# Transposed input of the later pairs: loaded in a second layout and normalised in place, or transposed on TensorE

## The chip, the cores and the metric

The kernel runs on one core of a Trainium2 chip. The metric is the device time of one execution in microseconds (us). Everything is float32. A core has five engines that run their own instruction streams: TensorE (PE in the profile, PEld for its weight loads), VectorE (DVE), ScalarE (ACT), GpSimd (POOL) and SyncE (SP), which here only issues DMA transfers.

## The reference

One transformer block over x of shape (8, 256, 512): 2048 tokens, each a row of 512 numbers.

```python
x = x + attention(layernorm(x), w_qkv, w_o)   # 32 query heads, 8 key/value heads, head size 128
x = x + ffn(layernorm(x), weight, bias, centroids, assignments)

def layernorm(x):          # over the last axis, no learned scale
    return (x - mean(x)) / sqrt(var(x) + 1e-5)

def attention(h, w_qkv, w_o):
    q, k, v = split(h @ w_qkv)
    scores = q @ k.T * 128 ** -0.5 - slope[head] * sqrt(i - j)   # causal: -inf where j > i
    return softmax(scores) @ v @ w_o

def ffn(h, ...):
    hits = softmax(h @ centroids.T / 0.1) > 0.01                 # 64 clusters
    dense = h @ weight.T + bias
    return where(any(hits, axis=1)[:, None] & any(hits, axis=0)[assignments][None, :], dense, 0)
```

## The kernel before

The eight sequences of the batch are taken two at a time. A pair is 512 tokens, held as four tiles of 128 tokens; there are four pairs, 0 to 3. Inside a pair the work goes by key/value head and by sequence: 8 heads times 2 sequences are 16 units, called slots 0 to 15 here (`slot = u % SPP`). A unit u computes the scores of its own head group; in the same stretch of instructions the unit before it has its maximum subtracted, its exponential taken and its rows summed, and the unit two back is multiplied with v and projected with w_o. The order on every engine is written out by hand (`manual_schedule`): the two long lines with `qq`, `e`, `x`, `w`, `rows` and `norm` in the body of the unit loop are that order, one for even slots (`bb == 0`) and one for odd slots. All matrix products with weights use Strassen's seven products, so GpSimd and VectorE also form sums of weight blocks (`a_sums`, `b_sums`).

TensorE contracts over the partition axis, so the projections of q, k and v need x with its 512 features on the partitions: `xT[p]`, a tile of 128 partitions by 4 feature chunks by 512 tokens. Before the change it comes about like this, for pair p + 1 while pair p is being worked on:

- slot 8: `load_x2` brings the four token tiles of the pair from memory (SP queue);
- slots 10 and 11: `norm(0)` to `norm(3)` treat two token tiles each. `norm_stats` (L259, L260, VectorE) gives mean and variance of each token, `norm_root` (L267, ScalarE) and `norm_scale` (L272, L274, VectorE) give `rstd` and `shift = -mean * rstd`, each one column with a token on each partition, and `norm_write` (L281, ScalarE) writes the normalised tile `xn`;
- slots 11 and 12: `x(0)` and `x(1)` call `norm_tile`, which transposes one normalised tile: four TensorE transposes into one PSUM bank (L290) and a ScalarE copy to `xT` (L291). Each of the two slots does two tiles, one before and one after `w(1)`;
- slots 13 and 14: `sum_x` (L125 to L131, VectorE) forms the Strassen sums of `xT`; slot 14 and 15 use it for the first projections of the next pair.

Four other steps of the same slots matter here. `sum_old` (L387, L388, L390, VectorE) reduces the rows of the exponentials; it comes right after `x(...)` in VectorE's order. `rows` transposes that result on TensorE (`tp_r`, L397), reduces it (L401, L404, VectorE), writes it to memory (`row_hbm`, L406, SP queue) and reads it back on all partitions (`bc`, L415, SP queue, two transfers). `subtract_max` uses `bc` on GpSimd (L422) and VectorE (L425), and `attend` uses it on VectorE (L450) for the result of `av`. After `attend`, `a_sums` forms the sums of `oT` on GpSimd (`o_s`, L112 to L118); at the end of an odd slot GpSimd also sums the next weights (L112 to L116 of `wq`, L125 and L129 of `wo`), in an even slot it finishes `wq_s` (L118).

Pair 0 goes through its own code ahead of the loop and is not touched by the change.

Of the kernel before, what the change touches and what calls it, by code (L numbers as in the profile page):

```python
# [14 lines left out]
F32 = mybir.dt.float32  # L15
I32 = mybir.dt.int32
AF = mybir.ActivationFunctionType
ALU = mybir.AluOpType
# [3 lines left out]
B, S, H = 8, 256, 512  # L22
# [3 lines left out]
P = 128  # L26
NC_H = H // P
PT_TOK = 2 * S
NPAIR = B // 2
# [24 lines left out]
def block_kernel(  # L54
    ctx: ExitStack,
    tc: tile.TileContext,
    x: bass.AP,
    w_qkv: bass.AP,
    w_o: bass.AP,
    w_ffn_t: bass.AP,  # L60
# [6 lines left out]
    nc = tc.nc  # L67
# [7 lines left out]
    work = ctx.enter_context(tc.tile_pool(name="work", bufs=1))  # L75
    small = ctx.enter_context(tc.tile_pool(name="small", bufs=4))
    dram = ctx.enter_context(tc.tile_pool(name="dram", bufs=4, space=bass.MemoryType.DRAM))
# [11 lines left out]
    gp, ve = nc.gpsimd.tensor_tensor, nc.vector.tensor_tensor  # L89
# [17 lines left out]
    def a_sums(tt, a, which="S1 S2 S3 S4"):  # L107
        for s in which.split():
            if callable(a[s]):
                a[s] = a[s]()  # L110
            if s == "S1":
                tt(a["S1"], a["A21"], a["A22"], ALU.add)  # L112
            elif s == "S2":
                tt(a["S2"], a["S1"], a["A11"], sub)
            elif s == "S3":
                tt(a["S3"], a["A11"], a["A21"], sub)  # L116
            else:
                tt(a["S4"], a["A12"], a["S2"], sub)  # L118
# [56 lines left out]
    def load_x2(t):  # L175
        x2[t] = work.tile([P, H], F32, tag="x2", name=f"x2_{t}", bufs=X2_BUFS)
        nc.sync.dma_start(x2[t], xf[ts(t, P), :])
# [75 lines left out]
    def norm_stats(*tiles):  # L253

        n = len(tiles)
        mv = small.tile([P, 2, 2], F32, tag="mv", name="mv", bufs=2)[:, :n]
        for j, t in enumerate(tiles):
            stats = small.tile([P, 6], F32, tag="stats", name=f"stats_{t}")
            nc.vector.bn_stats(stats, x2[t])  # L259
            nc.vector.bn_aggr(mv[:, j], stats)  # L260
        return mv, tiles
# [24 lines left out]
    def transpose_into(dst, xn, t, tp=None, copy=nc.scalar.copy):  # L286
        if tp is None:
            tp = p_tp.tile([P, 512], F32, tag="tp", name=f"tpx_{t}")
        for c in range(NC_H):
            nc.tensor.transpose(tp[:, ts(c, P)], xn[:, ts(c, P)], ident)  # L290
        copy(dst, tp.rearrange("p (c q) -> p c q", c=NC_H))  # L291

    xT = {}
    xB = {}

    def norm_tile(p, i, **kw):

        if i == 0:
            xT[p] = work.tile([P, NC_H, PT_TOK], F32, tag="xT", name="xT", bufs=2)
        t = p * TPP + i  # L300
        transpose_into(xT[p][:, :, ts(i, P)], xn_sb[t], t, **kw)

    def sum_x(p, which):

        if p in xB:
            b_sums(ve, xB[p], which)
            return
        s = work.tile([P, 3, 2, S], F32, tag="xT_t", name="xT_t")
        xB[p] = b_side([xT[p][:, 2 * k : 2 * k + 2, ts(n, S)] for k in range(2) for n in range(2)],
                       *(s[:, j] for j in range(3)))  # L310
        b_sums(ve, xB[p], which)
# [12 lines left out]
    def project_k(p, j):  # L324

        kT = kT_sb[p, j] = work.tile([P, 2, PT_TOK], F32, tag="kT", name="kT", bufs=2)
        return strassen("k", "aw", wk[p, j], xB[p],
                        lambda w, x: [(slice(0, S), w[:, c, :], x[:, c, :]) for c in range(2)],
                        [kT[:, m, ts(n, S)] for m in range(2) for n in range(2)], S)

    def project_q(g):

        qT = qT_sb[g] = work.tile([P, G, PT_TOK], F32, tag="qT", name="qT", bufs=2)
        v = qT.rearrange("p (e m) t -> p e m t", m=2)
        return strassen("q", "aq", wq[g], xB[g // NKV],
                        lambda w, x: [(ts(e, S), w[:, c, e, :], x[:, c, :]) for e in range(2) for c in range(2)],
                        [v[:, :, m, ts(n, S)] for m in range(2) for n in range(2)], 512)
# [167 lines left out]
    def ffn_transpose(t, tag="xnT", **kw):  # L505
        xnT_sb[t] = work.tile([P, NC_H, P], F32, tag=tag, name=f"xnT_{tag}")
        transpose_into(xnT_sb[t], xn_sb[t], t, **kw)
# [119 lines left out]
    k, q = project_k(0, 0), project_q(0)  # L627
# [15 lines left out]
    found = None  # L643

    for u in range(NU + 2):
        g, bb = divmod(u, 2)
        p, kv = divmod(g, NKV)
        slot = u % SPP
        own, old, out_ = u < NU, 0 < u <= NU, u >= 2
        more_q, more_p = own and g + 1 < NG, own and p + 1 < NPAIR  # L650
# [14 lines left out]
        e, qq = nothing, nothing  # L665
        if own and slot in (0, 1, 8, 9):
            e = project_v(p, slot // 8, bb)
        elif own and slot in (3, 7, 11):
            e = project_k(p, (slot + 1) // 4)
        elif more_p and slot == 15:  # L670
            e = project_k(p + 1, 0)
        if more_q:
            if bb == 0:
                q = project_q(g + 1)
            qq = q
        ww = {}

        def w(*steps):
            for i in steps:
                if out_:  # L680
                    if i == 1:
                        ww[0] = project_out(u - 2)
                    ww[0](i)
# [8 lines left out]
        def f(part):  # L692
            if t_ffn is not None:
                if part == 0:
                    ffn_transpose(t_ffn)
                elif part == 1:
                    ffn_logits(t_ffn)
                    ffn_exp(t_ffn)
                    ffn_dense(t_ffn, w_ffn)
                elif part == 2:  # L700
                    ffn_bias_add(t_ffn, y_late[:, t_ffn % TPP, :] if t_ffn >= first_late else None)
                else:
                    ffn_hits(t_ffn)
                    ffn_qsel(t_ffn)
                    ffn_end(t_ffn)


        t_norm = None
        if more_p and slot in (10, 11):
            t_norm = (p + 1) * TPP + 2 * (slot - 10)  # L710
        elif own and p > 0 and slot in (2, 4) and p < NPAIR - 1:
            t_norm = (p - 1) * TPP + slot - 2
        elif u in (NU - 3, NU - 1):
            t_norm = (NPAIR - 2) * TPP + u - (NU - 3)

        def norm(part):
            nonlocal found
            if t_norm is not None:
                found = (lambda _: norm_stats(t_norm, t_norm + 1), norm_root, norm_scale, norm_write)[part](found)

        def max_and_old():
            scores(u, 2)
# [14 lines left out]
        def sum_old():  # L737
            if old:
                over_keys(s_sb[u - 1], r, 1, ALU.add)
# [20 lines left out]
        def av(i):  # L760
            if out_:
                attend(u - 2, i)
                if i == 1:
                    a_sums(gp, o_sb[u - 2][1])

        def x(i):
            if more_p and slot in (11, 12):
                norm_tile(p + 1, 2 * (slot - 11) + i)

        if bb == 0 and own:  # L770
            qq(1), e(1), max_and_old(), e(2), f(0), av(0), e(6), exp_old(), av(1), more_sums(), rows_max(), f(1), e(7), qq(2)
            if u == 4:
                onehot_of_columns(asg)
            f(2), norm(0), e(5), e(4), qq(6), e(3), x(0), w(1), x(1), sum_old(), w(5, 6), norm(1), qq(7), w(2)
            rows(), behind_rows(), w(7, 3), norm(3), w(4)
        elif u < NU - 1:
            e(1), qq(4), e(2), max_and_old(), f(0), e(6), av(0), exp_old(), e(7), av(1), f(1), e(5), qq(5)
            f(2), norm(0), e(4), e(3), x(0), w(1), x(1), sum_old(), w(5, 6), norm(1), qq(3), w(2)
            rows(), behind_rows(), w(7, 3), norm(3), w(4)
        elif own:  # L780

            max_and_old(), f(0), av(0), exp_old(), av(1), rows_max(), f(1)
            f(2), norm(0), w(1), sum_old(), w(5, 6), norm(1), w(2)
            rows(), subtract_max(u, 0), subtract_max(u, 1)
            f(3), norm(2), w(7)
            nc.scalar.activation(s_sb[u], s_sb[u], AF.Exp)
            w(3), norm(3), w(4)
        elif bb == 0:
            sum_old(), av(0), av(1), f(0), rows(), f(1), w(1, 5), f(2), w(6, 2, 7, 3, 4), f(3)
        else:  # L790
            av(0), f(0), av(1), f(1)
            normalise(norm_stats(last, last + 1), tags=("y", "y"))
            ffn_hits(t_ffn), ffn_qsel(t_ffn)
            w(1), f(2), w(2, 5, 6)
            ffn_transpose(last)
            w(3)
            found = norm_root(norm_stats(last + 2))
            ffn_transpose(last + 1, "snap")
            w(7)
            norm_write(norm_scale(found))  # L800
            ffn_logits_product(last), ffn_logits_product(last + 1)
            w(4)
# [30 lines left out]
        if more_p and slot == 8:  # L833
            for i in range(TPP):
                load_x2((p + 1) * TPP + i)

        if u == 2:
            asg = load_assignments()
# [2 lines left out]
        if u == NU - 1:  # L841

            for i, (tag, pool) in enumerate((("xT", work), ("wq", wpool))):
                both = []
                for hbm in (x2_hbm[i], y_hbm[i]):
                    t = pool.tile([P, TPP, H], F32, tag=tag, name=f"back_{tag}", bufs=2)
# [45 lines left out]
    n = 0  # L892
    for t in range(NT):
        if t in SPLIT:
            continue
        p, i = divmod(t, TPP)
# [32 lines left out]
```

## Time and profile before

| | |
|---|---|
| median of 3 runs | 1440.6 us (1440.53 to 1444.04) |
| the profiled execution | 1441.13 us, its span 1439.4 us |
| TensorE busy | 1407.5 us, 98% of the span |
| VectorE busy | 928.2 us, 64% |
| GpSimd busy | 878.2 us, 61% |
| ScalarE busy | 372.2 us, 26% |
| granted TensorE clock, mean | 0.996 |
| DMA | 189.94 MB, 132 GB/s on average |

Busy time is the sum of the spans of an engine's instructions. Idle time of an engine that does not set the end costs nothing. A timeline row gives the start in us from the span's start, the time in us, the engine, the line of the kernel, the operation, what it writes and reads, the shapes, and in square brackets how long the engine had been idle before it and which instruction ended that.

### The profile page before, as it was taken

How to read it: one execution, taken by the hardware profiler on the slowest of the kernel's cores; microseconds unless marked ns; L12 is line 12 of the kernel's file. 1: busy time of each engine (PE TensorE's matmuls, PEld its weight loads, DVE VectorE, ACT ScalarE, POOL GpSimd, SP SyncE). 2: the span in 40 equal slices, each digit the busy share in tenths (PEclk: the TensorE clock that was granted, in tenths of full speed). 3: DMA queues.
4: the chain of work that ended last, by engine and by line, in shares of the span. 5: the costliest groups of instructions: out<-in, count | busy, mean ns of one | idle time of the engine just before them, and what ended most of it. 6: DMA issues, size and time to landing. Idle time of an engine off the chain costs nothing.

```text
span 1439.4 us, 16533 instructions
## 1 busy us (share of the span) xinstructions
PE 1407.5 (98%) x5859; PEld 1072.9 (75%) x5859; DVE 928.2 (64%) x1708; ACT 372.2 (26%) x650; POOL 878.2 (61%) x883
## 2 busy tenths in 40 slices
PE   8899999999999999999999999999999999999986
PEld 7677777767877777777777677787777777877663
DVE  5457666686556665667655666566756676556766
ACT  2222223411232222332213312142222211222332
POOL 6377857676464754667555466566747666466543
PEclk9999999999999999999999999999999999999998
DMA  5235433443242544424242425434323353243343
GB/s 190 88 122 176 132 115 136 146 147 132 89 161 74 176 144 150 161 98 142 98 147 102 167 83 176 153 126 147 132 90 117 132 176 132 89 162 103 101 149 117
DMA packets 85968, 189.94 MB, mean 132 GB/s; under 512 B 10592, under 2 KB 18784, under 8 KB 85888
## 3 DMA queue, kind: packets, MB, share of 16 engines
q1 hardware_dynamic: 84736, 186.41, 37.5%
q10 hardware_dynamic: 864, 1.57, 0.3%
q8 instruction: 47, 0.77, 0.2%
q0 software_dynamic: 288, 0.92, 0.2%
q14 instruction: 33, 0.27, 0.1%
HBM read 175.77 MB, written 13.11 MB: 131 GB/s over the span
## 4 chain that ended last, share of the span: by engine, by line
PE 90%; DVE 6%; issue 1%; ACT 1%; POOL 1%; DMA 1%; DVEq 0%; POOLq 0%; ACTq 0%; SPq 0%
PE ps_qa L145 14%; PE ps_oa L468 14%; PE ps_oc L468 7%; PE sc L370 7%; PE ps_qc L145 7%; PE av L446 7%; PE sc L376 4%; PE ps_ob L468 4%; PE ps_ka L145 4%; PE ps_va L145 4%; PE av L447 3%; PE ps_qb L145 3%; PE ps_f L546 3%; PE ps_kc L145 2%; PE ps_vc L145 2%
## 5 line engine op out<-in xcount | busy, mean ns | idle before, releaser
L500 POOL TENSOR_TENSOR x<-x,snap 128x256 f32<-128x256 f32 x189 | 136.0, 736 | 177.5 <-DVE x L488 105.1
L422 POOL TENSOR_TENSOR s<-s,bc 128x1024 f32<-128x1024 f32 x64 | 151.7, 2370 | 150.2 <-DMA bc<-row_hbm 150.0
L387 DVE TRANSPOSE_TENSOR_REDUCE r<-s 128x32 f32<-128x1024 f32 x128 | 158.0, 1234 | 4.5 <-ACT s L735 4.5
L112 POOL TENSOR_TENSOR o_s<-oT 128x256 f32<-128x256 f32 x64 | 47.6, 744 | 180.3 <-DVE oT L450 176.3
L158 ACT COPY qT<-ps_qa 128x512 f32<-128x512 f32 x128 | 74.8, 584 | 289.7 <-PE ps_qa L145 289.6
L483 ACT COPY snap<-ps_oa 128x256 f32<-128x256 f32 x189 | 70.4, 373 | 277.8 <-PE ps_oa L468 277.8
L468 PE MATMUL ps_oa<-wo,oT 128*128 128x256 f32 x512 | 132.7, 381 | 2.6 <-DVE oT L450 2.6
L735 ACT ACTIVATE s<-s 128x1536 f32<-128x1536 f32 x63 | 93.5, 1484 | 148.5 <-DVE s L425 137.8
L446 PE MATMUL av<-s,v 128*128 128x512 f32 x256 | 130.7, 592 | 0.0
L145 PE MATMUL ps_qa<-xT,wq 128*128 128x256 f32 x512 | 121.1, 379 | 0.8 <-ACT qT L158 0.8
L370 PE MATMUL sc<-qT,kT 128*128 128x512 f32 x256 | 120.3, 592 | 0.0
L145 PEld LDWEIGHTS ps_qa<-xT,wq 128*128 128x128 f32 x512 | 97.1, 190 | 27.8 <-issue 16.0
L372 DVE SCALAR_TENSOR_TENSOR s<-sc,alibi 128x512 f32<-128x512 f32 x128 | 88.0, 691 | 30.8 <-PE sc L370 29.8
L468 PEld LDWEIGHTS ps_oa<-wo,oT 128*128 128x128 f32 x512 | 90.9, 190 | 22.6 <-DVE oT L450 5.3
L378 DVE SCALAR_TENSOR_TENSOR s<-sc,alibi 128x512 f32<-128x512 f32 x64 | 44.3, 692 | 85.6 <-PE sc L376 85.6
L447 PEld LDWEIGHTS av<-s,v 128*128 128x128 f32 x256 | 48.6, 190 | 61.2 <-issue 61.2
L450 DVE TENSOR_TENSOR oT<-av,bc 128x512 f32<-128x512 f32 x128 | 83.9, 683 | 11.8 <-PE av L447 10.5
L388 DVE TRANSPOSE_TENSOR_REDUCE r<-s 128x16 f32<-128x512 f32 x128 | 85.6, 669 | 0.0
L447 PE MATMUL av<-s,v 128*128 128x256 f32 x256 | 76.1, 379 | 0.0
L488 DVE TENSOR_TENSOR x<-x,ps_ob 128x256 f32<-128x256 f32 x64 | 26.9, 421 | 73.2 <-PE ps_ob L468 73.1
L370 PEld LDWEIGHTS sc<-qT,kT 128*128 128x128 f32 x256 | 48.6, 190 | 33.9 <-issue 29.9
L494 DVE TENSOR_TENSOR x<-x,ps_oc 128x256 f32<-128x256 f32 x128 | 53.3, 416 | 30.5 <-PE ps_oc L468 29.6
(182 smaller groups left out, 2982.0 us busy)
## 6 DMA issues: line engine op xcount, KB each, us to landing
bc<-row_hbm SPq DMA_DIRECT2D x128, 512.0 KB, 4.8
wq<-in_w_qkv SPq DMA_DIRECT2D x32, 1024.0 KB, 7.7
wo<-in_w_o SPq DMA_DIRECT2D x32, 1024.0 KB, 7.8
alibi<-al_hbm SPq DMA_DIRECT2D x24, 512.0 KB, 8.4
wk<-in_w_qkv SPq DMA_DIRECT2D x16, 512.0 KB, 9.4
wv<-in_w_qkv SPq DMA_DIRECT2D x8, 1024.0 KB, 10.8
x<-in_x SPq DMA_DIRECT2D x16, 256.0 KB, 9.8
al_hbm<-alibi SPq DMA_DIRECT2D x8, 512.0 KB, 9.2
```

Of the source, the lines that this page charges most:

```text
L145: nc.tensor.matmul(bank[:, cols], lhsT=lhsT, rhs=rhs, start=first and j == 0, stop=j == len(mms) - 1, skip_group_check=True)
L370: nc.tensor.matmul(sc, lhsT=kT[:, t0 : t0 + P], rhs=qT[:, hh : hh + 2, t0 : t0 + S], start=True, stop=True)
L372: nc.vector.scalar_tensor_tensor(s[:, hh * S : (hh + 2) * S], sc, D ** -0.5, bias[:, hh : hh + 2, :].rearrange("p h q -> p (h q)"), ALU.mu ...
L387: nc.vector.tensor_reduce(first, s[:, :K0].rearrange("p (j q) -> p j q", q=32), AX.X, op, apply_transpose=True)
L388: nc.vector.tensor_reduce(second, s[:, K0:].rearrange("p (j q) -> p j q", q=32), AX.X, op, apply_transpose=True)
L422: gp(k0, k0, mx, sub)
L446: nc.tensor.matmul(av, lhsT=v[:, i0, vc], rhs=pT[:, hh * S : (hh + 2) * S], start=True, stop=False)
L447: nc.tensor.matmul(av3[:, :, P:S], lhsT=v[:, i0 + 1, vc], rhs=pT[:, K0 + hh * P : K0 + (hh + 2) * P].rearrange("p (h q) -> p h q", h=2), s ...
L450: ve(oT[:, e].rearrange("p k m q -> p k (m q)"), av3, inv[:, hh : hh + 2, :], ALU.mult)
L468: nc.tensor.matmul(bank[:, :HH], lhsT=x[:, e, :], rhs=y[:, e, :], start=first and e == 0, stop=e == 1, skip_group_check=True)
L500: gp(c, c, s, ALU.add)
L735: nc.scalar.activation(s_sb[u - 1], s_sb[u - 1], AF.Exp)
```

## The change

The host passes a second copy of x, `x_t`, in the layout of `xT`: for each pair 128 partitions by 4 feature chunks by 512 tokens. For pairs 1 to 3 the raw transposed x is loaded into `xT` by one 1 MB transfer in slot 8. Since a token is now a column of `xT`, its `rstd` and `shift` are needed as rows on every partition: `norm_rows` takes the place of `norm_write`, writes the two columns to memory with one DMA each (two tiles of 128 tokens, so 256 numbers each) and reads both back on all partitions as `norm_bc` with a third DMA. `norm_half` then normalises 256 tokens of `xT` in place: a multiplication on GpSimd, issued in slots 11 and 12 after the sums of `oT`, and an addition on VectorE, issued where `x(0)` stood, just before `sum_old`. The four transposes, the PSUM bank and the copy per tile go away for these pairs, as do their normalised tiles `xn`.

```diff
+    def load_xT(p):
+        xT[p] = work.tile([P, NC_H, PT_TOK], F32, tag="xT", name="xT", bufs=2)
+        nc.sync.dma_start(xT[p], x_t[p])
+
+    rows_bc = {}
+
+    def norm_rows(found):
+        tiles, rstd, shift = found
+        hbm = dram.tile([2, 2, P], F32, tag="norm_hbm", name="norm_hbm", bufs=2)
+        for k, col in enumerate((rstd, shift)):
+            nc.sync.dma_start(hbm[k].rearrange("j p -> p j"), col)
+        to = rows_bc[tiles[0] // 2] = work.tile([P, 2, S], F32, tag="xn", name="norm_bc", bufs=2)
+        nc.sync.dma_start(to.rearrange("p k t -> p (k t)"), hbm.rearrange("k j p -> (k j p)").partition_broadcast(P))
+
+    def norm_half(p, n, k):
+        x, bc = xT[p][:, :, ts(n, S)], rows_bc[p * 2 + n][:, k]
+        (gp, ve)[k](x, x, bc.unsqueeze(1).to_broadcast([P, NC_H, S]), (ALU.mult, ALU.add)[k])
...
-                found = (lambda _: norm_stats(t_norm, t_norm + 1), norm_root, norm_scale, norm_write)[part](found)
+                write = norm_rows if slot in (10, 11) and more_p else norm_write
+                found = (lambda _: norm_stats(t_norm, t_norm + 1), norm_root, norm_scale, write)[part](found)
...
                 if i == 1:
                     a_sums(gp, o_sb[u - 2][1])
+                    if more_p and slot in (11, 12):
+                        norm_half(p + 1, slot - 11, 0)
-        def x(i):
+        def x():
             if more_p and slot in (11, 12):
-                norm_tile(p + 1, 2 * (slot - 11) + i)
+                norm_half(p + 1, slot - 11, 1)
...
-            f(2), norm(0), e(4), e(3), x(0), w(1), x(1), sum_old(), w(5, 6), norm(1), qq(3), w(2)
+            f(2), norm(0), e(4), e(3), x(), w(1), sum_old(), w(5, 6), norm(1), qq(3), w(2)
             rows(), behind_rows(), w(7, 3), norm(3), w(4)
...
             for i in range(TPP):
                 load_x2((p + 1) * TPP + i)
+            load_xT(p + 1)
...
+        "x_t": np.ascontiguousarray(
+            np.asarray(inputs["L0_attn_hidden_states"]).reshape(NPAIR, PT_TOK, NC_H, P).transpose(0, 3, 2, 1)),
```

The line of the even slots changes in the same way.

More of the change, by code (lines that the diff above doesn't have):

```diff
@@ L57, in block_kernel @@
     x: bass.AP,
+    x_t: bass.AP,
     w_qkv: bass.AP,
@@ L773, in block_kernel @@
                 onehot_of_columns(asg)
-            f(2), norm(0), e(5), e(4), qq(6), e(3), x(0), w(1), x(1), sum_old(), w(5, 6), norm(1), qq(7), w(2)
+            f(2), norm(0), e(5), e(4), qq(6), e(3), x(), w(1), sum_old(), w(5, 6), norm(1), qq(7), w(2)
             rows(), behind_rows(), w(7, 3), norm(3), w(4)
```

## The prediction

> **What bounds the kernel now.** I read the page's busy times and its chain of waits first, then the timelines of TensorE, VectorE and GpSimd in the slots that the change touches.
>
> ```profile
> PE 1407.5 (98%) x5859; PEld 1072.9 (75%) x5859; DVE 928.2 (64%) x1708; ACT 372.2 (26%) x650; POOL 878.2 (61%) x883
> ...
> PE 90%; DVE 6%; issue 1%; ACT 1%; POOL 1%; DMA 1%; DVEq 0%; POOLq 0%; ACTq 0%; SPq 0%
> ...
> L422 POOL TENSOR_TENSOR s<-s,bc 128x1024 f32<-128x1024 f32 x64 | 151.7, 2370 | 150.2 <-DMA bc<-row_hbm 150.0
> ```
>
> TensorE is busy for 98% of the span and is 90% of the chain: what it no longer does is won, and what it has to wait for is lost. So two things count: what the transposes cost TensorE, and whether the new GpSimd and VectorE work makes it wait. TensorE's timeline in slots 11 and 12 of pair 1 (the transposes are those of pair 2):
>
> ```profile
> 613.74 0.60 PE L290 MATMUL tpx<-ident,xn 128*128 128x128 f32 x4
> 614.18 1.03 PE L468 MATMUL ps_oa<-wo,oT 128*128 128x256 f32 x4
> 615.05 0.63 PE L290 MATMUL tpx<-ident,xn 128*128 128x128 f32 x4
> ...
> 619.83 0.27 PE L397 MATMUL tp_r<-ident,r 128*64 128x128 f32 x1
> ...
> 632.87 0.60 PE L290 MATMUL tpx<-ident,xn 128*128 128x128 f32 x4
> 633.31 1.03 PE L468 MATMUL ps_oa<-wo,oT 128*128 128x256 f32 x4
> 634.22 0.65 PE L290 MATMUL tpx<-ident,xn 128*128 128x128 f32 x4
> ...
> 639.03 0.27 PE L397 MATMUL tp_r<-ident,r 128*64 128x128 f32 x1
> ```
>
> No row has an idle time in brackets: TensorE runs through. VectorE in the same slots:
>
> ```profile
> 614.44 0.39 DVE L168 TENSOR_TENSOR kT<-kT,ps_kc 128x256 f32<-128x256 f32 x1
> 614.74 1.24 DVE L387 TRANSPOSE_TENSOR_REDUCE r<-s 128x32 f32<-128x1024 f32 x1
> ...
> 616.61 0.53 DVE L390 TENSOR_TENSOR r<-r 128x16 f32<-128x16 f32 x1
> ...
> 633.24 1.25 DVE L387 TRANSPOSE_TENSOR_REDUCE r<-s 128x32 f32<-128x1024 f32 x1 [1.10 <-ACT s L735]
> ...
> 635.11 0.70 DVE L390 TENSOR_TENSOR r<-r 128x16 f32<-128x16 f32 x1
> ```
>
> L390 ends at 617.14 and 635.81; `tp_r`, which reads it, starts at 619.83 and 639.03. The slack is 2.7 us in slot 11 and 3.2 us in slot 12. That is what the change has to fit into. GpSimd:
>
> ```profile
> 612.58 0.73 POOL L118 TENSOR_TENSOR o_s<-oT,o_s 128x256 f32<-128x256 f32 x1
> 613.26 1.27 POOL L112 TENSOR_TENSOR wq_s<-wq 128x512 f32<-128x512 f32 x1
> ...
> 615.84 1.26 POOL L116 TENSOR_TENSOR wq<-wq 128x512 f32<-128x512 f32 x1
> ...
> 633.81 0.73 POOL L118 TENSOR_TENSOR o_s<-oT,o_s 128x256 f32<-128x256 f32 x1
> 634.50 1.28 POOL L118 TENSOR_TENSOR wq_s<-wq,wq_s 128x512 f32<-128x512 f32 x1
> ```
>
> GpSimd goes from the `o_s` sums into weight sums without a gap. The multiplication goes between these two.
>
> **What is removed.** Per later pair four groups of four transposes. From the first row of a group to the next instruction: 0.44 (613.74 to 614.18), 0.46, 0.44 and 0.49 us, together 1.83 us; three pairs, 5.5 us off TensorE. ScalarE loses 12 copies (0.59 us) and 12 normalisations (0.76 us); at 26% busy it is late for nobody in these rows, so I take 0.
>
> **What is added, slot 11.** The multiplication has 128x1024 numbers, as L422: 2.37 us. No row shows a multiplication with a repeated operand; bounds are 2.1 us (three L500 rows of 0.70) and 3.4 us (four L347 rows of 0.85); L422 has its width, so 2.37. It starts when S4 is done (613.3) and ends at 615.65. VectorE, free at 614.83, waits for it with the addition, and in order behind that stand L387, L388 and L390, for which TensorE's `tp_r` waits.
>
> Does the addition start at 615.65? How the two engines share shows in L390, 0.18 us when GpSimd is idle: at 616.61 it took 0.53 and ended at 617.14, just after GpSimd's L116 (615.84 + 1.26 = 617.10). A VectorE instruction with two SBUF inputs also waits in the sums of `xT`:
>
> ```profile
> 1006.61 1.65 DVE L125 TENSOR_TENSOR xT_t<-xT 128x512 f32<-128x512 f32 x1
> ...
> 1006.45 1.26 POOL L125 TENSOR_TENSOR wo_t<-wo 128x512 f32<-128x512 f32 x1
> 1007.78 1.60 POOL L129 TENSOR_TENSOR wo<-wo 128x512 f32<-128x512 f32 x1
> ```
>
> VectorE's L125 ends at 1008.26, 0.55 us after GpSimd's first row (1007.71), and the second takes 1.60 instead of 1.27. Each waits for the other's whole instruction. GpSimd's next sum starts with no gap, before the semaphore can reach VectorE (0.09 us between L450's end and L112), so I let the addition wait for one more GpSimd instruction: 1.27 us, to 616.9. The addition itself is twice the 0.55, 1.1 us, to 618.0 (other end: 1.24, as L387 of that width). [...]
>
> L387 and L388 take 1.83 us (614.74 to 616.57): 619.85. L390 meets GpSimd's L116, now 619.3 to 620.6, and ends at 620.6. `tp_r` could start at 619.83 - 0.90 = 618.9 without the transposes. TensorE stands for 1.7 us; net of the transposes slot 11 loses 0.8. VectorE then has L494, L168 and L488 to do before L401, so the write of `row_hbm` comes 2.2 us after `tp_r` instead of 1.5: `bc`, L422, L425, L450 and the `o_s` sums of slot 12 are 0.7 later against TensorE. `w(1)` needs L450 (ends at 631.54) and would start at 632.87 without the first transposes: 1.3 us to spare, so 0.
>
> **Slot 12.** In TensorE's time: the `o_s` sums end at 634.54, the multiplication at 636.9, GpSimd's L118 (1.28) at 638.2, the addition at 639.3, L387 and L388 at 641.1, L390 at 641.25; plus the 0.7: 641.95. `tp_r` is ready at 639.03 - 0.93 = 638.1. TensorE stands for 3.85 us; net 2.9 lost. Slot 13 keeps some 0.2 of lateness. Sum: 0.8 + 2.9 + 0.2 = 3.9 per pair; in pair 0 the instruction behind the multiplication is L347 (0.85) instead of L118, 0.4 less: 3 x 3.9 - 0.4 = 11.3 us. On the profiled execution's 1441.1 that is 1452.4; it stands 0.5 over the median, so 1452 of the median's scale. A multiplication at its upper bound (1.0 more in each of six slots) gives 1458, an addition of 1.24 under 1 more.
>
> The longest idle time that the trace shows for TensorE in the unit loop is 1.48 us, at a granted clock of 1.00. [...]
>
> **The transfers.** All are on SP's queue. `xT` (1 MB, three times) follows the x tiles of slot 8. The DMA windows of pair 0 show 335 GB/s until 222 us, then nothing until the row write at 228.85: 1 MB more is done by 226. Hidden; if not, slot 9's `bc` is late by up to 3 us. `norm_rows`: two column writes, then a wait on SP until they land, then the broadcast; behind that stand the loads of `wq`, `alibi`, `wv` (slot 10) and `wo` (slot 11). `wq` goes out some 6 us later, near 607, and lands (7.7) near 615, when GpSimd needs it (615.65, before 613.26): hidden, barely. `wo` is used a slot later. The broadcast for slot 12: `bc` is issued near 624.6 (1.7 after the row write, as now), the column writes behind it near 626; no row shows writes of 4 bytes. Lower bound as `row_hbm`, 1.7 us; upper bound four times that each (256 pieces against 64), 6.8. With the `bc` bytes ahead (4.8) and a broadcast of 1.7 to 4.8 the rows are there between 630 and 642; the multiplication wants them at 636. I take hidden, since `row_hbm` is the nearest row. At the upper end slot 12 loses 6 us, three times.
>
> **The rivals.**
> - Slack takes it all: the addition ends within 1.8 us (slot 11) and 2.3 us (slot 12) of where VectorE stands now, the slack less the transposes. Then only the 5.5 us count: 1435, faster. For it: 2.7 and 3.2 us of slack, VectorE at 64%. Against it: in slot 12 L387 would have to start by 635.5, and the multiplication starts at 634.5 and takes 2.37.
> - No wait for the next GpSimd instruction: slot 11 stands for 0.5 (L390 still meets L114), net 0.4 won; slot 12 stands for 2.6, net 1.7 lost; 0.2 after it. 1.5 a pair, 4.5: 1445.
> - The rows land late: a multiplication 1 to 6 us late in slot 12 of three pairs, on top of the forecast: 1455 to 1470.
>
> **How the numbers follow.** Forecast 1452 with its bounds (1448 to 1458): 0.52. No second wait, 1443 to 1447: 0.2. Late rows: 0.18. All in the slack: 0.1. The range 1441 to 1461 leaves out the slack case and the upper half of the late rows. A measurement of this kernel tells 0.3% (4.3 us) from no change. Slower by more: the forecast, late rows and half of the second rival, 0.8; within it 0.1; faster 0.1.
>
> **What would show it.** In the changed profile: `tp_r` of slots 11 and 12 of pairs 0 to 2 with idle times near 1.7 and 3.9 us, released by DVE r L390; the addition at about 2.4 us in its row (1.27 waiting); GpSimd's sums after it stretched by some 1.1; no L422-like multiplication that waits for norm_bc. If those `tp_r` rows have no idle time the sum is wrong from its first step; if the multiplication waits for a DMA, the late rows have it; idle times of 0.5 and 2.6 mean no second wait.

## The result, and the profile after

The changed kernel takes 1481.65 us (median of 6 runs, 1477.2 to 1484.49) against 1440.53 us for the kernel before (median of 6, 1438.85 to 1444.04). The ratio is 1.0277, with a 95% interval of 1.0262 to 1.0291. It is slower, as forecast, but by 41 us and not by 11: the time lies 30 us above the forecast and 21 us above the end of the range. The profiled execution took 1484.19 us, its span is 1482.2 us.

The page first: the busy times, the granted clock in tenths over the span, and the chain of waits.

```profile
PE 1422.6 (96%) x5811; PEld 1080.6 (73%) x5811; DVE 936.7 (63%) x1714; ACT 356.2 (24%) x626; POOL 896.3 (60%) x889
...
PEclk9999999999999999989999999998999999999999
...
PE 79%; DVE 8%; DMA 8%; POOL 2%; issue 2%; ACT 1%; SPq 0%; POOLq 0%; DVEq 0%; ACTq 0%
```

Two readings come out of the first line. TensorE was idle for 1482.2 - 1422.6 = 59.6 us, where it had been idle for 1439.4 - 1407.5 = 31.9 us before: 27.7 us of new waiting. And it was *busy* for 15.1 us longer, although 48 transposes worth some 5.5 us are gone. So about 20.6 us are instructions that took longer than before. The two together are the 42.8 us of the span. The mean granted clock fell from 0.996 to 0.983, and two slices in the middle of the clock line now show 8, where before only the last one did. In the chain, DMA went from 1% to 8%.

The table of waits says who waited for whom (engine, tile and line, releaser, total us, times, longest):

```profile
DVE xT L323 <- POOL xT L323: 28.9, 6, 9.4
...
PE tp_r L419 <- DVE r L412: 25.1, 11, 6.7
...
DVE oT L472 <- DMA bc<-row_hbm: 18.4, 6, 4.8
POOL xT L323 <- DMA norm_bc<-norm_hbm: 13.9, 6, 4.7
PE ps_oa L490 <- DVE oT L472: 6.7, 2, 3.6
...
PE ps_qc L146 <- DVE oT L472: 5.7, 2, 3.2
```

The row of `tp_r` stood at 5.6 us in 5 times before (other slots), so the six new ones cost 19.5 us. The two rows in which TensorE waits for L472, the result of `attend`, stood at 2.6 us before, so they cost 9.8 us more. Together that covers the 27.7 us of new waiting. Behind them stand two waits that were in no term of the forecast's sum: `attend` waits 18.4 us for its `bc` (1.3 us before), and the multiplication waits for the rows in all six slots. In what follows, an idle time of TensorE is called a stand. TensorE's timeline in slots 11 and 12 of pair 1, with the idle time and its releaser in brackets:

```profile
624.37 3.21 PE L146 MATMUL ps_qc<-xT_t,wq_s 128*128 128x256 f32 x8 [2.53 <-DVE oT L472]
...
652.01 1.83 PE L490 MATMUL ps_oa<-wo,oT 128*128 128x256 f32 x4 [3.59 <-DVE oT L472]
...
658.12 1.03 PE L490 MATMUL ps_ob<-wo,oT 128*128 128x256 f32 x4
663.38 0.42 PE L419 MATMUL tp_r<-ident,r 128*64 128x128 f32 x1 [4.24 <-DVE r L412]
663.60 1.93 PE L490 MATMUL ps_oa<-wo,oT 128*128 128x256 f32 x4
```

In slot 12 TensorE stands twice: 3.59 us for L472, which waits for `bc`, and 4.24 us for the row sums. The four matmuls of L490 take 1.83 and 1.93 us after a stand; four of the same shape take 1.03 us at 658.12. The windows (busy time of PE, PEld, DVE, ACT, POOL, then the granted clock, the DMA share and GB/s) show it as the clock:

```profile
660.00:665.00 5.00, 1.61 (x5) 1.34 (x6) 4.78 (x9) 0.00 (x0) 1.01 (x2) 0.75 0.00 2
665.00:670.00 5.00, 5.00 (x13) 3.50 (x12) 0.84 (x2) 0.37 (x1) 1.41 (x2) 0.56 0.45 130
670.00:675.00 5.00, 5.00 (x18) 3.14 (x17) 2.83 (x4) 0.59 (x1) 2.35 (x1) 1.00 1.03 384
```

The clock was granted at 0.75, then at 0.56, and is back at 1.00 at 670. In pair 0, where `tp_r` waits 3.45 and 6.71 us, the windows from 270 and from 298 us each show 0.50. In slots 11 and 12 of the three pairs the trace has the clock at 0.50 for 41.0 us in all, in eight stretches of 3.4 or 6.8 us; TensorE is busy for 36.2 us of them. At the full clock that work would take half as long: an estimate of 18 us lost, which is most of the 20.6.

The transfers behind it, in the list of DMA issues for 609 to 625 us (KB each, median us from issue to landing; a transfer has landed when its completion is reported):

```profile
bc<-row_hbm SPq DMA_DIRECT2D x2, 512.0 KB, 8.1
norm_hbm<-rstd SPq DMA_DIRECT2D x1, 1.0 KB, 11.7
```

A column write of 1 KB lands after 11.7 us, where the row write `row_hbm` takes 1.7. Of the two `bc` transfers issued just ahead of it, one landed in its usual time and the other with the columns, hence the 8.1; the same stretch of the kernel before has 4.7. In slot 12 the two landed after 4.2 and 11.8 us. The bytes are moved long before: from 612 to 616 us the DMA share is 0.9 and more, from 616 to 617 us it is 0.08, and from 616.5 to 623.5 us the trace has not one packet. The late `bc` lands at 623.5 us, the columns at 623.7 and 623.8. So for 7 us nothing is moved on the DMA engines that the profile traces, and only the completions are outstanding.

**Theory A**: writing the columns 4 bytes at a time is slow and holds up the `bc` issued ahead of it; late `bc`, late rows and the arithmetic queue one behind the other in front of `tp_r`, and the long stands bring the clock down. **Rival B**: the arithmetic alone is dearer than forecast (GpSimd's multiplication, the wait on VectorE). **Rival C**: SP, blocked until the columns land, sends the weights late.

### The profile page after: what moved, and what is told of

Read it like the earlier page. It is cut to its first block, busy times and chain, and to the rows that moved or that the text cites. A ratio compares the mean times of both kernels' runs of the same rounds, so it can differ in the third digit from the quotient of the medians.

```text
span 1482.2 us, 16486 instructions
## 1 busy us (share of the span) xinstructions
PE 1422.6 (96%) x5811; PEld 1080.6 (73%) x5811; DVE 936.7 (63%) x1714; ACT 356.2 (24%) x626; POOL 896.3 (60%) x889
## 4 chain that ended last, share of the span: by engine, by line
PE 79%; DVE 8%; DMA 8%; POOL 2%; issue 2%; ACT 1%; SPq 0%; POOLq 0%; DVEq 0%; ACTq 0%
PE ps_oa L490 13%; PE ps_qa L146 12%; PE ps_oc L490 7%; PE sc L392 7%; PE ps_qc L146 6%; PE av L468 5%; DMA norm_hbm<-shift 5%; PE ps_va L146 4%; PE sc L398 3%; PE ps_ob L490 3%; PE ps_f L568 3%; PE ps_ka L146 3%; PE ps_qb L146 3%; PE av L469 3%; DMA norm_bc<-norm_hbm 2%; PE ps_vc L146 2%
## 5 line engine op out<-in xcount | busy, mean ns | idle before, releaser
L490 PE MATMUL ps_oa<-wo,oT 128*128 128x256 f32 x512 | 138.1, 393 | 6.7 <-DVE oT L472 6.7
L490 PEld LDWEIGHTS ps_oa<-wo,oT 128*128 128x128 f32 x512 | 93.4, 195 | 28.0 <-DVE oT L472 10.8
L472 DVE TENSOR_TENSOR oT<-av,bc 128x512 f32<-128x512 f32 x128 | 83.9, 683 | 28.1 <-DMA bc<-row_hbm 18.4
L490 PE MATMUL ps_oc<-wo_t,o_s 128*128 128x256 f32 x256 | 68.6, 391 | 2.7 <-POOL o_s L113 2.5
```

The source lines that it names most:

```text
L472: ve(oT[:, e].rearrange("p k m q -> p k (m q)"), av3, inv[:, hh : hh + 2, :], ALU.mult)
L490: nc.tensor.matmul(bank[:, :HH], lhsT=x[:, e, :], rhs=y[:, e, :], start=first and e == 0, stop=e == 1, skip_group_check=True)
```

## The experiments

Medians are of 4 to 6 runs; ratios are to the kernel before on the same chip in the same session.

**1. Transfers only.** The multiplication and the addition are left out.

```diff
-                    if more_p and slot in (11, 12):
-                        norm_half(p + 1, slot - 11, 0)
...
-            if more_p and slot in (11, 12):
-                norm_half(p + 1, slot - 11, 1)
```

> The changed kernel with the multiplication and the addition left out (the transposed x stays unnormalised); all its transfers stay: the 1 MB loads, the column writes and the broadcasts. Theory A (the column writes hold up the transfer issued before them, and TensorE stands for that): in pairs 1 and 2 VectorE's multiplication of av still waits some 4 to 5 us for bc in slots 11 and 12, TensorE stands 2.5 to 3.6 us each time and its clock falls after it; time 1435 plus about 20, so 1450 to 1460. Theory B (the arithmetic on GpSimd and VectorE is the whole cost): no stand in slots 11 and 12, 5.5 us of transposes less, 1435.

Measured: 1449.29 us, ratio 1.0065 (1.0041 to 1.0088). TensorE's stands in slots 11 and 12 of pair 1:

```profile
614.59 3.42 PE L146 MATMUL ps_qc<-xT_t,wq_s 128*128 128x256 f32 x8 [3.07 <-DVE oT L472]
...
640.25 1.30 PE L490 MATMUL ps_oa<-wo,oT 128*128 128x256 f32 x4 [2.29 <-DVE oT L472]
```

With no arithmetic at all, TensorE waits for `attend`, which waits for `bc`; `tp_r` does not wait in these slots. Without the transposes and with nothing added the kernel would stand near 1435, so the transfers alone cost some 14 us, a little less than A expected. That is against B as the whole story. C can be read here too: GpSimd waits 16.4 us for `wq`, which SP sends late (1.0 us before), but no matmul waits for a sum of weights, neither here nor in the changed kernel; one weight load does, for 0.9 us in the changed kernel and in two cases of together 1.7 us before and here. C is true of GpSimd and costs TensorE next to nothing.

**2. Arithmetic only.** No column is written; `norm_bc` is broadcast from a row of x, so the values are not the norms, with sizes and instructions kept.

```diff
-        hbm = dram.tile([2, 2, P], F32, tag="norm_hbm", name="norm_hbm", bufs=2)
-        for k, col in enumerate((rstd, shift)):
-            nc.sync.dma_start(hbm[k].rearrange("j p -> p j"), col)
...
-        nc.sync.dma_start(..., hbm.rearrange("k j p -> (k j p)").partition_broadcast(P))
+        nc.sync.dma_start(..., xf[tiles[0], :].partition_broadcast(P))
```

> The changed kernel without the column writes: the broadcast takes one row of x in place of the norms (so the values are not the norms), everything else stays. Theory A: bc is no longer late and the stands at av's result are gone; what is left is the addition ahead of the row sums, TensorE standing 0.5 to 1.7 us at tp_r in slot 11 and 2.6 to 3.9 in slot 12: 1445 to 1455. Theory B: nearly all of the loss stays, 1470 to 1482.

Measured: 1447.28 us, ratio 1.0048 (1.003 to 1.0066). Slots 11 and 12 of pair 1:

```profile
621.47 0.30 PE L416 MATMUL tp_r<-ident,r 128*64 128x128 f32 x1 [1.29 <-DVE r L409]
...
643.49 0.30 PE L416 MATMUL tp_r<-ident,r 128*64 128x128 f32 x1 [3.37 <-DVE r L409]
```

The forecast had 1.7 and 3.85. Pair 2 has 1.28 and 3.36 us, pair 0 1.29 and 2.26; the six are 12.8 us, where the forecast had 16.3. Its arithmetic is right in mechanism and a little too large in size. B falls: neither part alone accounts for 41 us.

**3. The columns turned into rows first.** `rstd` and `shift` lie in one tile of four columns; one TensorE transpose (`tp_n`) and a ScalarE copy make four rows of 512 bytes, and one DMA writes them. Everything else is as in the change.

```diff
...
+        tp = p_tp.tile([P, 512], F32, tag="tp", name="tp_n")
+        nc.tensor.transpose(tp[:4, :P], both, ident)
+        rows4 = work.tile([4, P], F32, tag="y", name="rows4", bufs=2)
+        nc.scalar.copy(rows4, tp[:4, :P])
-        for k, col in enumerate((rstd, shift)):
-            nc.sync.dma_start(hbm[k].rearrange("j p -> p j"), col)
+        nc.sync.dma_start(hbm.rearrange("k j p -> (k j) p"), rows4)
```

> The changed kernel with the two columns of each half turned into rows by one small TensorE transpose and written with one DMA of four rows of 512 bytes. Theory A: that write lands in about 2 us instead of 11, bc is not held up, the norms are there before the multiplication; the time is that of the arithmetic alone, 1445 to 1455, a little above the run without column writes. Theory B: 1470 to 1482, as before.

Measured: 1451.82 us, ratio 1.0079 (1.0064 to 1.0094). On SP's queue, slot 11 of pair 1:

```profile
629.74 0.33 SPq L320 DMA_DIRECT2D norm_hbm<-rows  x1
633.50 0.33 SPq L322 DMA_DIRECT2D norm_bc<-norm_hbm  x1
```

The broadcast, which waits for the write, goes out 3.8 us after it; in the changed kernel it is 12.3 us (639.94 to 652.22). The wait of the multiplication for its rows is gone, and that of `attend` for `bc` is down from 18.4 us to 1.6. Some 29 of the 41 us, by the ratios, hang on the shape of one small write.

**4. TensorE kept busy.** The changed kernel, with 18 matmuls of ones ahead of `tp_r` in slot 12, where TensorE would stand.

```diff
+        if u < NU and u % SPP == 12 and u // SPP + 1 < NPAIR:
+            for _ in range(18):
+                nc.tensor.matmul(tp[:, 256:384], lhsT=ones, rhs=ones, start=True, stop=True)
```

> The changed kernel with 18 small matmuls of constants (some 3.9 us, their result is not used) on TensorE just ahead of tp_r in slot 12 of pairs 0 to 2, where it stands 4.2 to 6.7 us. If the granted clock falls because TensorE stands, the work behind tp_r goes at full speed again (2.7 us to the next scores instead of 5.3): about 8 us less than the changed kernel, 1472 to 1476. If the clock has another cause, or the loss is not there, 1481 or more.

Measured: 1476.8 us, ratio 1.0251 (1.0232 to 1.027), just above the range expected. More work, and 5 us faster, though the interval touches that of the change (1.0262 to 1.0291). Pair 1, slot 12, where the 18 matmuls have just taken 4.18 us:

```profile
659.25 0.30 PE L422 MATMUL tp_r<-ident,r 128*64 128x128 f32 x1 [1.91 <-DVE r L412]
659.39 1.06 PE L493 MATMUL ps_oa<-wo,oT 128*128 128x256 f32 x4
```

L493 (the same matmuls as L490 in the changed kernel) takes 1.06 us and not 1.93, and the windows from 660 to 670 us have a clock of 1.00. The mean clock rose from 0.983 to 0.991. In pair 0 it is the same; in pair 2 TensorE still stood for 2.51 us behind the added matmuls, and the next ones were as slow as in the changed kernel (1.35, 1.91 and 1.63 us). TensorE was busy for 1426.1 us, of which the added matmuls are about 3 x 4.18; without them 1413.6, 9 us less than in the changed kernel. So filling a stand keeps the clock up. The 9 us are no price of slot 12 alone: in this execution `bc` landed up to 1.7 us earlier, `attend` waited 10.6 us for it and not 18.4, and with that other stands were shorter too.

**5. The column writes on ScalarE's DMA queue.**

```diff
-            nc.sync.dma_start(hbm[k].rearrange("j p -> p j"), col)
+            nc.scalar.dma_start(hbm[k].rearrange("j p -> p j"), col)
```

> The changed kernel with the column writes issued on ScalarE's DMA queue in place of SP's; the broadcast stays on SP and still waits for them. If the second bc is held up by standing ahead of the column writes in the same queue: bc lands in 4 to 5 us everywhere, VectorE no longer waits for it in slots 11 and 12 of pairs 1 and 2, and the time falls by the stands and the slow clock behind them, to 1458 to 1468. If the transfers hold each other up whatever the queue: bc still lands after 11 to 12 us and the time stays at 1478 to 1484.

Measured: 1485.34 us, ratio 1.0303 (1.0283 to 1.0322). The medians of the writes are still 10.2 and 11.2 us, and `bc` on SP's queue, now issued 1 to 3 us after them, is still late: all twelve in slots 10 and 11 of the three pairs take 11.7 to 14.6 us, in pair 0 too. Now VectorE's part of `subtract_max` waits for it, where it had waited 0.2 us once:

```profile
DVE s L447 <- DMA bc<-row_hbm: 35.0, 7, 7.2
```

What holds `bc` up is therefore not the order on one queue.

**6 and 7. Columns that nobody reads, 4 bytes and 512 bytes apart.** Both write the columns as the change does and feed `norm_bc` from a row of x, so the values are not the norms and nothing waits for the columns. In the second each number lies 512 bytes from the next in memory: the same 512 pieces of 4 bytes, spread out.

```diff
-        hbm = dram.tile([2, 2, P], F32, ...)
+        hbm = dram.tile([2, 2, P, P], F32, ...)
-            nc.sync.dma_start(hbm[k].rearrange("j p -> p j"), col)
+            nc.sync.dma_start(hbm[k, :, :, 0].rearrange("j p -> p j"), col)
```

> The changed kernel with the column writes kept, but the broadcast takes a row of x, so that no instruction waits for the column writes (the values are not the norms). If the part of the loss that neither the transfers alone (1449) nor the arithmetic alone (1447) shows is the wait of the multiplication for its late rows: the two losses against 1434.5 add up, 14.8 + 12.8, to 1462. If it is the held-up bc together with the clock, 1475 to 1482.

> As the run in which nothing reads the column writes, but every number is written 512 bytes from the next instead of 4 (512 pieces of 4 bytes as before, not the norms either). If the writes are slow because many 4-byte pieces go to the same few hundred bytes of memory: they land in 4 to 5 us, bc is not held up, the time falls to that of the arithmetic alone, 1447. If it is the number of pieces: they land in 9 to 12 us and the time is that of the run with 4 bytes apart.

Measured: 1470.96 us (ratio 1.0209, 1.019 to 1.0229) with 4 bytes, in neither of the two ranges expected, 1448.89 us (1.0047, 1.003 to 1.0064) with 512 bytes. The DMA issues of the one and then of the other:

```profile
norm_hbm<-rstd SPq DMA_DIRECT2D x6, 1.0 KB, 12.2
```

```profile
norm_hbm<-rstd SPq DMA_DIRECT2D x6, 1.0 KB, 5.2
```

The same number of pieces lands in less than half the time once they are apart, the wait of `attend` for `bc` goes from 23.5 us to 0.9, and the time is that of the arithmetic alone (1447.28). Two points weigh against a simple story. First, 1471 us without anyone waiting for the columns: the writes do most of their harm by holding up *other* transfers (`norm_bc` from x itself landed after 12.0 us, and after 5.5 with the spacing). Second, the reader's wait, and SP's with it, are the rest, 10 us by the ratios.

**8. 64 bytes apart.** As the last, with a spacing of 64 bytes.

```diff
+        hbm = dram.tile([2, 2, P, 16], F32, ...)
```

> The columns written but read by nobody, each number 64 bytes from the next in memory (4 bytes apart it took 1471 us and the writes 12 us; 512 bytes apart 1449 us and 5 us). The broadcast of the norms is fed by a row of x, so the values are not the norms. If writes that meet in a line of 64 bytes are what is slow: 5 us and 1446 to 1452. If the line is larger (up to 512 bytes): 8 writes of a line still meet, the writes take between 6 and 12 us, and the time lies between 1452 and 1471.

Measured: 1449.54 us, ratio 1.0052 (1.0035 to 1.0069); the writes land in 5.3 and 5.1 us. 64 bytes do what 512 do. So pieces side by side are slow, and pieces 64 bytes apart are not; spacings between the two were not tried. Whether what counts is that no two pieces meet within 64 bytes, or that all of them lie spread over 32 KB and not 2, these runs do not separate.

**9. The addition behind the rows, columns as in the change.** `sum_old` and `tp_r` no longer stand behind the addition on VectorE.

```diff
 # in x()
-            if more_p and slot in (11, 12):
-                norm_half(p + 1, slot - 11, 1)
...
 # in behind_rows()
             norm(2)
+            if more_p and slot in (11, 12):
+                norm_half(p + 1, slot - 11, 1)
```

> The change, columns written as in it, but the addition stands in VectorE's order behind the row sums and the instructions that follow them, so that tp_r waits neither for the multiplication nor for the addition. Theory A (the lateness of the transfers and of the arithmetic stand one behind the other on VectorE, in front of tp_r, and the clock falls on the long stands): without the arithmetic in that place only the held-up bc remains, so close to the run without the arithmetic, 1448 to 1455, idle times of tp_r under 1 us, clock 0.99 or more. Rival (the late rows cost by themselves, because SP stands and GpSimd's queue stands behind the multiplication): 1460 or more, with GpSimd's late multiplication now late for the sums of oT and of wq.

Measured: 1455.54 us, ratio 1.0096 (1.0081 to 1.0111), mean clock 0.994. The waits:

```profile
POOL xT L323 <- DMA norm_bc<-norm_hbm: 16.2, 6, 4.6
DVE oT L472 <- DMA bc<-row_hbm: 15.0, 7, 4.2
...
PE tp_r L419 <- DVE r L412: 5.6, 5, 1.6
```

The rows are as late as ever (16.2 us), `bc` too, yet `tp_r` is back at its 5.6 us of before and 26 us are won. The time lies half a microsecond above what A expected, by the ratios some 4 us above the run without arithmetic. There TensorE waited for GpSimd's `o_s` for 3.1 us in all, here for 5.7: the late multiplication pushes GpSimd's own sums.

**10. Both mended: rows written as rows, addition behind the rows.** As in 3, with the addition moved as in 9, and `norm(3)` with its small transpose behind `w(4)` in slots 10 and 11.

> The run with rows made by TensorE, with two more changes: the addition stands behind the row sums and tp_r instead of ahead of them, and the small transpose stands behind the last product of the slot, when shift is ready. If the sum of the prediction is right where the transfers are out of it, VectorE's and TensorE's slack behind tp_r takes the addition, no stand is left in slots 11 and 12, and the 5.5 us of transposes (less 0.7 for six small ones) show: 1434 to 1437. If the addition delays the next scores all the same: 1440 to 1446.

Measured: 1435.0 us (median of 6, 1433.27 to 1436.35), ratio 0.9954 (0.994 to 0.9968), 0.5% below the kernel before. Slots 11 and 12 of pair 1:

```profile
615.90 0.27 PE L423 MATMUL tp_r<-ident,r 128*64 128x128 f32 x1
...
634.85 0.27 PE L423 MATMUL tp_r<-ident,r 128*64 128x128 f32 x1
```

No idle time in either; TensorE is busy for 1401.6 us, 5.9 us less than before. This is the gain that the removed transposes had to offer, and the rest of the change hides.

Put side by side, as ratios to the kernel before:

| | addition ahead of the row sums | addition behind them |
|---|---|---|
| columns written 4 bytes apart | 1.0277 | 1.0096 |
| rows written as rows | 1.0079 | 0.9954 |

From the corner at 0.9954, the columns alone cost 1.42%, the place of the addition alone 1.25%, both together 3.23%: 0.56%, some 8 us, more than the sum. The small transpose is in the lower row only, so the comparison between the rows holds it too; it also stands later in the order in experiment 10, and its waits of together 2.3 us in experiment 3 are gone there. TensorE's times in five profiled executions say where the excess sits:

| | span | TensorE busy | TensorE idle |
|---|---|---|---|
| before | 1439.4 | 1407.5 | 31.9 |
| change | 1482.2 | 1422.6 | 59.6 |
| addition behind (9) | 1453.0 | 1408.4 | 44.6 |
| rows as rows (3) | 1450.3 | 1409.0 | 41.3 |
| both (10) | 1431.3 | 1401.6 | 29.7 |

Over the last row the busy time is 6.8 and 7.4 us longer for one fault and 21.0 for both, while the idle time adds up (14.9 + 11.6 against 29.9, 3.4 more). The clock says the same: TensorE was busy at 0.50 for 10.2 us in slots 11 and 12 of experiment 9, for 10.2 in experiment 3, for 36.2 in the change, and for none in experiment 10; the mean granted clock was 0.994, 0.994, 0.983 and 0.997. Half of that busy time is what it cost, 5.1, 5.1 and 18.1 us (an estimate), so most of the excess is matmuls at the lower clock. Either fault brings the clock down; the longer stands of both together do so more often and for longer.

## Why the prediction was wrong

- **What is removed** was right: 5.9 us less busy time in experiment 10, against 5.5.
- **What is added, slots 11 and 12** held as a step. The multiplication takes 2.35 us (2.37 forecast). The addition took 2.27 us where it met a sum on GpSimd, and 1.23 us in the slots where GpSimd's next sum was itself waiting for its weights (in slot 12 of pair 0 the next instruction is the making of `alibi`, L369, and the addition took 1.23 us as well), all in the changed kernel:

```profile
631.37 1.23 DVE L323 TENSOR_TENSOR xT<-xT,norm_bc 128x1024 f32<-128x1024 f32 x1 [1.13 <-POOL xT L323]
...
659.10 2.27 DVE L323 TENSOR_TENSOR xT<-xT,norm_bc 128x1024 f32<-128x1024 f32 x1 [5.95 <-POOL xT L323]
```

  So the wait that the sum added for one more GpSimd instruction is there: where it met a sum on GpSimd, the addition took 2.27 - 1.23 = 1.04 us more (1.27 forecast). In experiment 2, where GpSimd has its weights, five of the six additions took 2.27 us. The stands of 1.29 and 3.37 us there answer 1.7 and 3.85, and the whole of it gives 1447 where the sum had 1452. The rival "no second wait" names 1447 too, as the end of its span, but by a mechanism that did not happen.
- **The transfers** are the step that failed: "I take hidden, since `row_hbm` is the nearest row." The row write of 8 KB was near in size and not in kind. The twelve writes take 9.2 to 12.7 us, 11.7 in the median, above even the upper bound of 6.8, which was scaled by the number of pieces; experiments 6 to 8 show that the number is not what counts. The sentence named the price if the cover was gone, 6 us in slot 12 alone; the multiplication waited in all six slots, 13.9 us together.
- **Missing altogether** was that a small write can hold up its neighbour: no step asked what happens to the `bc` issued ahead of the columns. It is behind the 14 us of experiment 1, and behind 23 us by the ratios where the arithmetic follows it (experiment 6 against 7).
- **The clock** was in no term of the sum: the longest idle time of TensorE in the unit loop before is 1.48 us, at a clock of 1.00. It came to some 18 of the 20.6 us of longer busy time. A stand of 3.85 us, which the sum itself forecast, is 2.6 times the longest that the trace could price, reason enough to make room for it in the range. The windows have 0.50 with stands of 3.45 and 6.71 us, 0.56 behind 4.24, and 1.00 where matmuls had filled the stand. Below 3.5 us the length of a stand alone does not settle it in these runs. Behind the 3.07 us of experiment 1 eight matmuls took 3.42 us, and the same eight 1.89 us elsewhere in that run; behind a stand of 1.65 us there, a group of four matmuls still took 1.91 us that takes 1.03 us elsewhere. Behind the 3.37 us of experiment 2 in pair 1 the next two such groups took 1.07 and 1.03 us, behind the 3.36 us in pair 2 they took 1.46 and 1.91. Each of the 15 stands of 3.5 us or more in the timelines of the change and of experiments 1 to 7 and 10 was followed by slow matmuls: 1.91 to 2.08 us for a group of four that takes 1.03, or 3.51 to 3.78 us for the eight that take 1.89.
- **The rival "the rows land late"** named the right transfers and one of their two harms; the larger one, the held-up `bc`, was not in it. At 1455 to 1470 it was too cheap by 12 us, for the two reasons above, and its chance of 0.18 was too low for a cost that no row of the trace could bound.
- **The slack** could not take the arithmetic in the place where it stood, but it could one step later: "slack takes it all: 1435" is what experiment 10 measures.

## What to carry to other kernels

Look at the shape of a small write before its size: columns written number by number, side by side into memory, took some 12 us here and delayed the transfers around them, and one small transpose ahead of the write took that away. Work that may be late belongs behind the short instructions that the critical engine waits for, not ahead of them: moving one addition was worth 26 us beside the slow writes and 18 us without them. Two delays that meet in one stand of TensorE cost more than their sum here: stands of 3.5 us and more were always followed by matmuls that took up to twice as long (2.08 us where 1.03 is usual), shorter ones only in part.

## What the runs showed of the hardware

- 512 pieces of 4 bytes onto 2 KB of memory land in 11.6 and 11.8 us in the median of the two writes (9.2 to 12.7 for single writes); with 64 or 512 bytes between them in 5.0 to 5.3 us in the median; as four rows of 512 bytes the next transfer that waits for them is issued after 3.8 us. In slot 11 of pair 1 the last packet of the slow ones starts at 616.4 us and they land at 623.7 and 623.8; between 616.5 and 623.5 us there is no packet at all.
- Such writes hold up a transfer that was issued just before them (11.3 to 12.7 us instead of 4 to 5), or one issued after them on another queue (11.7 to 14.6 us; VectorE stood up to 7.2 us for it). In the changed kernel this happened in pairs 1 and 2 and not in pair 0, whose `bc` (4.0 to 5.1 us) landed in time beside column writes of 9.2 to 11.3 us. What differs there was not found.
- With both on SP's queue it is always the second of the two `bc` transfers that is held up, the one issued about half a microsecond before the writes; the first lands after 3.9 to 4.2 us in the changed kernel. Why stays open; the runs show only when each was moved and when it completed.
